# The first attention of a twelve-block network: which operand is stationary in the product with the values

## The chip, the cores and the metric

The kernel runs on one core of a Trainium2 chip. The metric is the time of one execution on the device in microseconds (us), lower is better. The core has a matrix engine (TensorE, in profiles PE, with its weight loads shown apart as PEld), three engines for element-wise work (VectorE or DVE, ScalarE or ACT, GpSimd or POOL), and a queue for transfers (SyncE or SP). A matrix multiplication has a stationary operand, which is loaded into the array as weights, and a moving one, which is streamed through it; the result goes to PSUM.

## The reference

A stream `x` of 4 batches, 128 tokens and 128 features passes twelve residual blocks. The change is in the first, which attends from the tokens to 4 x 2048 context rows. Cut to what matters here (`bitnet_linear` multiplies quantized activations by ternary weights):

```python
vis = bitnet_linear(dinov2_features, W_d2v, b_d2v)             # the context, (4, 2048, 96)
image_embeds = bitnet_linear(vis, W_img, b_img)                # (4, 2048, 128)
fused = bitnet_linear(text_embeddings, W_txt, b_txt)           # the normalized stream, (4, 128, 128)
for Wa, ba in ((W_att0, b_att0), (W_att1, b_att1)):
    kv = bitnet_linear(image_embeds, Wa, ba)                   # 64 features
    k = jnp.concatenate([kv, kv], axis=-1)
    scores = jnp.einsum('bse,bpe->bsp', fused, k) * inv_sqrt_e
    attn = jax.nn.softmax(scores, axis=-1)
    fused = fused + 0.1 * jnp.einsum('bsp,bpe->bse', attn, k)
avg_img = jnp.mean(image_embeds, axis=1, keepdims=True)
concatenated = jnp.concatenate([fused, jnp.broadcast_to(avg_img, (b, s, e))], axis=-1)
h = jax.nn.relu(bitnet_linear(concatenated, W_f1, b_f1))
return bitnet_linear(h, W_f2, b_f2)
```

Keys and values are the same 64 features, used twice side by side to make 128.

## The kernel before, in words

The program is written with a tile framework: each block is a Python method, each engine has an instruction queue that is worked in order, and buffers come from pools that reuse a tag's buffers in turn. A reader of a buffer therefore holds up whoever is given that buffer next. A scheduler settles the order of the instructions of one engine from the order of the code.

`bit_attention` (L771) is the first block. L819 to L897 quantize and project the context. For each round r they leave in one large tile `kv` the keys `kT` (64 features of even and odd chunks of 128 keys on the two halves of the partitions, L886 to L890) and the values `v`: per chunk of 128 keys 64 columns and a 65th column of ones, which L875 sets on GpSimd (once per round) and which L896 leaves alone when it copies the 64 columns out of PSUM.

The attention then runs over eight units (`Unit`, L899), two rounds times four batches. A unit has these steps:

- `queries` (L909): L911 folds the two halves of `fused` on TensorE, L913 scales the result to `fq` on VectorE, L914 adds a bias to `fused`.
- `scores(g)` (L918), for the two halves g = 0, 1 of the keys: 8 products of keys and queries (L924), two at a time on the two halves of the array's rows, into a PSUM tile `st` of 128 keys x (8 chunks x 128 queries); L926 takes the maximum over the chunks on VectorE.
- `top` (L928) and `spread` (L935): L929, L931 and L933 take the maximum over all keys and partitions, by way of a transpose on TensorE; L936 is the second transpose, which spreads it; ScalarE copies the result to `mb` (L938).
- `weights(g)` (L940): VectorE subtracts the maximum out of PSUM (L942), ScalarE takes the exponential in place (L944). The probabilities `p`, with keys on partitions, come from a pool of three buffers.
- `values` (L947): 16 products (L953), one a chunk of keys. The probabilities of a chunk, 128 keys x 128 queries, are the stationary operand and the chunk's 65 columns of values and ones move through. The result `av` has queries on partitions, and its 65th column holds the sum of the weights. L957 takes the reciprocal of that column (128x1), L959 multiplies and doubles the columns, L961 transposes on TensorE and L962 adds to `fused`.

L969 to L995 set the order: in step i the code takes the maximum of unit i, the first half of the scores of unit i+1, the exponentials of unit i, the products with the values of unit i-1, the second half of the scores of unit i+1, and the queries of unit i+2. In step 2 the ternary weights of the later layers are made (`ternary`, L790, whose temporaries L804 have the tag `qtmp` in a pool of two buffers). In steps 3 and 4 one half of a mask each is read by a transfer (L989, into a tile of the same tag `qtmp`) and converted on GpSimd (L992, 3 partitions of 4096 columns). The small PSUM tiles of all these steps (`fq_ps`, `m_tr`, `av`, `o_tr`) share one tag `mm` with two buffers; the score tiles have three.

After the last unit, L1002 takes the largest magnitude of `fused`; its last step is a reduction over the partitions on GpSimd (L749, `am_f_g`)[...]. The program changes the library[...] (in the trace, a pair of MODIFY_POOL_CONFIG records at L341, L749 and L992).

Of the kernel before, what the change touches and what calls it, by code (L numbers as in the profile page):

```python
# [9 lines left out]
F32 = mybir.dt.float32  # L10
# [4 lines left out]
ALU = mybir.AluOpType  # L15
# [3 lines left out]
P = 128  # L19
B = 4  # L20
T = 128
# [3 lines left out]
NS = B * S  # L25
DC = 96
NCH = S // P
# [233 lines left out]
def bc_mid(ap, n):  # L261

    return ap.unsqueeze(1).to_broadcast([ap.shape[0], n, ap.shape[1]])
# [7 lines left out]
class Net:  # L271
# [499 lines left out]
    def bit_attention(self, nxt):  # L771


        nc, tc = self.nc, self.tc
        w = self.load("l0x")
        with ExitStack() as es:
            one = es.enter_context(tc.tile_pool(name="bit1", bufs=1))
            wk = es.enter_context(tc.tile_pool(name="bit2", bufs=2))
            big = es.enter_context(tc.tile_pool(name="bit_big", bufs=2))
            BIG = NS // 2 + B * NCH * 65  # L780
            qp = es.enter_context(tc.tile_pool(name="bit_q", bufs=1))
            tp = es.enter_context(tc.tile_pool(name="bit_t", bufs=3))

# [30 lines left out]
            ps = es.enter_context(tc.tile_pool(name="bit_ps", bufs=2, space=PSUM))  # L814
# [29 lines left out]
            total = one.tile([P, NS // W], F32, name="total")  # L844
# [24 lines left out]
            HC = NCH // 2  # L869
            rounds = []  # L870
            for r, n in enumerate(("att0", "att1")):
                kv = big.tile([P, BIG], F32, tag="big", name="kv")
                kT = kv[:, 0 : NS // 2]
                v = kv[:, NS // 2 :].rearrange("p (c w) -> p c w", w=65)
                nc.gpsimd.memset(v[:, :, 64:65], 1.0)  # L875
                osc = out_scale(n, s_img)
                osc10 = self.small(1, "osc10" + n)
                nc.vector.tensor_scalar_mul(osc10, osc, 0.1)
                rounds.append((n, kT, v, osc10))
                pairs = qimg.rearrange("p (c h k) -> p c h k", h=2, k=P)  # L880
                for j in range(B):
                    mm = stp.tile([P, W], F32, tag="st", name="k_ps")
                    for lo in range(0, W, 512):
                        at = (j * W + lo) // P
                        for h in range(2):
                            nc.tensor.matmul(  # L886
                                mm[h * 64 : h * 64 + 64, lo : lo + 512], qw[:, L0X[n]], pairs[:, at : at + 4, h],
                                start=True, stop=True)
                    nc.scalar.activation(
                        kT[:, j * W : j * W + W], mm, AF.Identity, bias=self.col("b_" + n), scale=osc)  # L890
                    mm = stp.tile([P, W], F32, tag="st", name="v_ps")
                    for i in range(NCH):
                        at = (j * NCH + i) * P
                        nc.tensor.matmul(
                            mm[:, i * 64 : i * 64 + 64], qimg[:, at : at + P], qw[:, L0X[n]], start=True, stop=True)
                    nc.vector.tensor_copy(  # L896
                        v[:, j * NCH : j * NCH + NCH, 0:64], mm.rearrange("p (c w) -> p c w", w=64))  # L897

            class Unit:  # L899

# [8 lines left out]
                def queries(u):  # L909
                    mm = ps.tile([P, 512], F32, tag="mm", name="fq_ps")  # L910
                    nc.tensor.matmul(mm[:, 0:T], self.flat(fold), u.fb, start=True, stop=True)  # L911
                    u.q = wk.tile([P, T], F32, tag="fq", name="fq")
                    nc.vector.tensor_scalar_mul(u.q, mm[:, 0:T], 1.0 / math.sqrt(C))  # L913
                    nc.vector.scalar_tensor_tensor(  # L914
                        u.fb, self.col("b_" + u.n).to_broadcast([P, T]), 0.1, u.fb, ALU.mult, ALU.add)
                    u.mh = wk.tile([P, 2, P], F32, tag="mh", name="mh")

                def scores(u, g):  # L918
                    u.st[g] = stp.tile([P, 2, HC // 2, P], F32, tag="st", name="st")
# [20 lines left out]
                def weights(u, g):  # L940
# [3 lines left out]
                    nc.scalar.activation(p, p, AF.Exp)  # L944
                    u.ts.append(p)

                def values(u):  # L947
                    av = ps.tile([P, 512], F32, tag="mm", name="av")
                    for g in range(2):
                        for h in range(2):  # L950
                            for c in range(HC // 2):
                                ch = u.b * NCH + 2 * (g * (HC // 2) + c) + h
                                nc.tensor.matmul(  # L953
                                    av[:, 0:65], u.ts[g][:, h * (HC // 2) + c], u.v[:, ch],
                                    start=g + h + c == 0, stop=g + h == 2 and c == HC // 2 - 1)
                    r = self.small(1, "rsum")
                    nc.vector.reciprocal(r, av[:, 64:65])  # L957
                    o = wk.tile([P, 2, 64], F32, tag="o", name="o")
                    nc.vector.tensor_scalar(o, bc_mid(av[:, 0:64], 2), r, u.osc10, ALU.mult, ALU.mult)  # L959
                    mm = ps.tile([P, 512], F32, tag="mm", name="o_tr")  # L960
                    nc.tensor.transpose(mm[:, 0:P], self.flat(o), self.ident)  # L961
                    nc.vector.tensor_add(u.fb, u.fb, mm[:, 0:P])  # L962

            units = [Unit(r, b) for r in range(2) for b in range(B)]
            units[0].queries()
# [969 lines left out]
```

## Time and profile before

| What | Value |
|---|---|
| median of 3 runs | 1716.02 us (1714.92 to 1716.68) |
| the profiled execution | 1714.14 us, of which the span 1712.3 us |
| TensorE busy | 1267.0 us, 74% of the span |
| VectorE, ScalarE, GpSimd busy | 1004.9, 624.2 and 140.3 us |
| L953, products with the values | 256 records, 52.9 us busy |
| L924, scores | 256 records, first at 82.4 us, last at 170.4 us |
| GpSimd between 93.2 and 181 us | two instructions, 7.5 us (L992) |

The profile is of one execution. Its page gives the busy time of each engine in forty equal slices; the chain of waits follows back from the last instruction what each one waited for; the timeline gives instructions in order of time, with how many of a kind follow one another; and a row of a group has a line of the code, the engine, the operation, what is written and read, the shape, the count, the busy time and the mean duration in ns. For a matmul, "128*64 128x512" means 128 rows and 64 columns of the array in use, and 512 columns streamed on 128 partitions. The windows view has for each stretch its length, then busy time and number of instructions for PE, PEld, DVE, ACT and POOL, then the clock that TensorE was granted (1.00 is full), the share of the transfer engines and GB/s.

The stage of the change in that view:

| Stretch, us | PE busy | DVE busy | granted clock |
|---|---|---|---|
| 93.2 to 97.5 | 4.30 | 1.57 | 0.87 |
| 104.5 to 111.7 | 7.20 | 3.58 | 0.50 |
| 134.5 to 141.5 | 7.00 | 3.52 | 0.50 |
| 155 to 162 | 6.11 | 3.15 | 0.50 |
| 181 to 188 | 6.91 | 0.34 | 0.50 |

### The profile page before, as it was taken

To read this page: it belongs to the slowest core of one execution; us is meant where nothing else is said; L and a number is where in the kernel's file an instruction comes from. 1 tells how busy PE (TensorE), PEld (TensorE's weight loads), DVE (VectorE), ACT (ScalarE), POOL (GpSimd) and SP (SyncE) were. 2 spreads that over 40 slices of the span, in tenths; PEclk is the share of its full clock that TensorE was granted. 3 is DMA by queue.
4 is the path that set the end of the run, shared out by engine and by line. 5 is a ranking of instruction groups with operands and counts; after the bars stand their busy time and mean duration, and the time that the engine had idled before them with its cause. 6 is when DMAs were issued, how large, how long until landed. Compare 5 with 4: busy or idle time off the path is not lost.

```text
span 1712.3 us, 15537 instructions
## 1 busy us (share of the span) xinstructions
PE 1267.0 (74%) x6142; PEld 675.3 (39%) x6142; DVE 1004.9 (59%) x1568; ACT 624.2 (36%) x796; POOL 140.3 (8%) x108
## 2 busy tenths in 40 slices
PE   2689547676999999999547155989658328899867
PEld 0378412224434444444213033744225214554544
DVE  8964468993256767676567843124448565444335
ACT  3722255552155656465333012315214202343332
POOL 0010014561000000000001000000012010000000
PEclk9965558798589999999759567959779558898878
DMA  5000000005000000000010004010000000000010
GB/s 153 1 1 1 0 0 5 21 1 155 1 24 1 0 1 1 0 1 1 0 49 1 0 0 123 5 36 0 0 2 1 9 0 1 1 2 2 6 47 7
DMA packets 9372, 28.19 MB, mean 16 GB/s; under 512 B 1176, under 2 KB 7105, under 8 KB 8143
## 3 DMA queue, kind: packets, MB, share of 16 engines
q1 hardware_dynamic: 8174, 24.88, 5.0%
q10 hardware_dynamic: 1120, 2.27, 0.4%
q8 instruction: 50, 0.82, 0.2%
q14 instruction: 28, 0.22, 0.0%
HBM read 26.88 MB, written 0.26 MB: 16 GB/s over the span
## 4 chain that ended last, share of the span: by engine, by line
PE 63%; DVE 24%; ACT 5%; issue 3%; POOL 3%; DMA 1%; POOLq 0%; ACTq 0%; DVEq 0%
PE av L518 12%; PE sc L492 12%; PE s_ps L638 3%; DVE na_m L643 3%; PE mm L1282 3%; PE av L953 3%; PE t_ps L662 3%; PE q_ps L438 2%; DVE h L1199 2%; PE h_ps L1631 2%; PE av L675 2%; PE y_ps L1638 2%; PE y_ps L1204 2%; PE st L924 2%; POOL hc L1202 1%
## 5 line engine op out<-in xcount | busy, mean ns | idle before, releaser
L518 PE MATMUL av<-s,ctx 128*97 128x512 f32 x448 | 211.1, 629 | 19.4 <-ACT s L516 19.3
L492 PE MATMUL sc<-q_aug,ctxT 99*128 99x512 f32 x448 | 207.5, 607 | 1.8 <-DVE q_aug L439 1.8
L494 ACT COPY s<-sc 128x1024 f32<-128x1024 f32 x112 | 113.0, 1010 | 95.2 <-PE sc L492 95.2
L518 PEld LDWEIGHTS av<-s,ctx 128*97 128x97 f32 x448 | 76.6, 174 | 146.9 <-issue 109.0
L515 DVE TENSOR_TENSOR s<-s,mbs 128x1024 f32<-128x1024 f32 x112 | 128.9, 1220 | 4.8 <-ACT mbs L512 4.8
L643 DVE TENSOR_REDUCE na_m<-s_ps 128x2 f32<-128x1024 f32 x64 | 75.7, 1220 | 89.2 <-PE s_ps L638 89.1
L492 PEld LDWEIGHTS sc<-q_aug,ctxT 99*128 99x128 f32 x448 | 83.8, 195 | 96.3 <-issue 79.2
L516 ACT ACTIVATE s<-s 128x1024 f32<-128x1024 f32 x112 | 113.5, 1053 | 10.8 <-DVE s L515 8.2
L498 DVE TENSOR_TENSOR m<-m,s 128x1024 f32<-128x1024 f32 x72 | 88.1, 1223 | 21.9 <-ACT s L494 20.7
L1204 PE MATMUL y_ps<-hc,consts 128*128 128x512 f32 x128 | 75.3, 723 | 33.6 <-POOL hc L1202 30.7
L668 ACT ACTIVATE p<-t_ps 128x1024 f32<-128x1024 f32 x64 | 62.1, 1021 | 91.3 <-PE t_ps L662 91.2
L529 DVE RECIPROCAL rsum<-y 128x2 f32<-128x2 f32 x40 | 6.6, 166 | 133.5 <-PE y L526 133.5
L1202 POOL TENSOR_TENSOR hc<-h,cs 128x1024 f32<-128x1024 f32 x32 | 77.5, 2431 | 86.3 <-DVE h L1199 86.0
L1199 DVE TENSOR_TENSOR_SCAN h<-dA,dbu 128x512 f32<-128x512 f32 x64 | 74.4, 1204 | 3.6 <-ACT dA L1196 3.4
L638 PE MATMUL s_ps<-kT,q 32*128 32x512 f32 x256 | 66.7, 734 | 1.9 <-ACT p L668 1.0
L341 POOL TENSOR_TENSOR ln_sq<-ln_xc 128x512 f32<-128x512 f32 (+1 forms) x19 | 23.3, 1225 | 537.9 <-DVE ln_xc L339 537.9
L662 PE MATMUL t_ps<-q,kT 32*128 32x128 f32 x1024 | 54.5, 319 | 8.8 <-DVE na_m L643 5.8
L1204 PEld LDWEIGHTS y_ps<-hc,consts 128*128 128x128 f32 x128 | 26.0, 222 | 83.2 <-POOL hc L1202 57.0
L662 PEld LDWEIGHTS t_ps<-q,kT 32*128 32x128 f32 x1024 | 45.0, 215 | 26.4 <-DVE na_m L643 14.7
L1196 ACT ACTIVATE dA<-delta,A 128x508 f32<-128x508 f32 x64 | 42.7, 688 | 33.1 <-DVE h L1199 32.2
L953 PEld LDWEIGHTS av<-kv,p 128*128 128x128 f32 x256 | 53.2, 319 | 0.2 <-issue 0.2
L953 PE MATMUL av<-kv,p 128*128 128x65 f32 x256 | 52.9, 399 | 0.0
(574 smaller groups left out, 2084.4 us busy)
## 6 DMA issues: line engine op xcount, KB each, us to landing
w_moe<-in_moe SPq DMA_DIRECT2D x2, 2048.0 KB, 8.0
ctxT<-in_ctxT SPq DMA_DIRECT2D x4, 768.0 KB, 14.7
rows<-in_rows ACTq DMA_DIRECT2D x1, 2048.0 KB, 11.8
w_l3f<-in_l3f SPq DMA_DIRECT2D x1, 1920.0 KB, 7.9
w_l0f<-in_l0f SPq DMA_DIRECT2D x1, 1024.0 KB, 4.8
w_mamba<-in_mamba SPq DMA_DIRECT2D x1, 976.0 KB, 20.5
w_r<-in_r SPq DMA_DIRECT2D x1, 960.0 KB
consts<-in_consts SPq DMA_DIRECT2D x1, 832.0 KB, 18.6
```

The costliest lines, as they stand in the source:

```text
L492: nc.tensor.matmul(sc[:, i], self.ctxT[:, at : at + P], qg, start=True, stop=True)
L494: nc.scalar.copy(s, sc)
L515: nc.vector.tensor_sub(p, p, bc_mid(mbs, 2))
L516: nc.scalar.activation(p, p, AF.Exp)
L518: nc.tensor.matmul(av[: DC + 1], self.ctx[:, b * NCH + chunks[j + i]], p[:, i], start=j + i == 0, stop=j + i == n - 1)
L638: nc.tensor.matmul(ts[g // 2][:, g % 2], qs[lo : lo + 32], kT[lo : lo + 32, s, j * 512 : j * 512 + 512], start=True, stop=True)
L643: nc.vector.tensor_reduce(part[:, at : at + 2], t, axis=AX, op=ALU.max, negate=True)
L662: nc.tensor.matmul(ts[g // 2][:, g % 2, j], kT[g * 32 : g * 32 + 32, s, at : at + P], qs[g * 32 : g * 32 + 32], start=True, stop=True)
L953: nc.tensor.matmul(av[:, 0:65], u.ts[g][:, h * (HC // 2) + c], u.v[:, ch], start=g + h + c == 0, stop=g + h == 2 and c == HC // 2 - 1)
L1199: nc.vector.tensor_tensor_scan(h[:, half], self.flat(dA), dbu[:, half], 0.0, ALU.mult, ALU.add)
L1202: nc.gpsimd.tensor_mul(hc, h, bc_mid(cs, 2))
L1204: nc.tensor.matmul(y[:, half], self.ident, hc[:, half], start=n == 0, stop=n == 15)
```

## The change

In `values` the operands swap places. A chunk's 64 columns of values become the stationary operand, and the probabilities move, 128 columns at a time. The product has features on partitions and queries along the free axis; chunks of h = 0 are summed on the lower 64 columns of the array, those of h = 1 on the upper 64, and the two alternate. The ones column and the two memsets that set it are gone, and with them 65 becomes 64 in the layout of `v`.

The sums of the weights are now made in two steps. In `weights`, three additions on GpSimd for each half g reduce the eight chunks of `p` to one 128x128 tile `total` (512, 256 and 128 columns; the intermediate has the tag `qtmp`). In `values`, two products with a matrix of ones sum `total` over the keys; every partition then holds the sums of all queries. The reciprocal is taken of this 128x128 tile, multiplied by `av`, and a product with `fold` adds the two halves of the columns and repeats the result on both halves of the partitions, so that no transpose is needed. The last instruction scales and adds to `fused`. In the scheduled order of TensorE, the transpose of the maxima (L931) now stands ahead of the first half of the next scores, where before two of those eight products stood ahead of it.

```diff
-            BIG = NS // 2 + B * NCH * 65
+            BIG = NS
...
-                v = kv[:, NS // 2 :].rearrange("p (c w) -> p c w", w=65)
-                nc.gpsimd.memset(v[:, :, 64:65], 1.0)
+                v = kv[:, NS // 2 :].rearrange("p (c w) -> p c w", w=64)
...
+                u.total = wk.tile([P, 2, P], F32, tag="total", name="total")
...
                     nc.scalar.activation(p, p, AF.Exp)
                     u.ts.append(p)
+                    half = p[:, 0 : HC // 2]
+                    a = wk.tile([P, HC // 2, P], F32, tag="qtmp", name="psum")
+                    nc.gpsimd.tensor_add(a, half, p[:, HC // 2 :])
+                    nc.gpsimd.tensor_add(a[:, 0:2], a[:, 0:2], a[:, 2:4])
+                    nc.gpsimd.tensor_add(u.total[:, g], a[:, 0], a[:, 1])
...
                 def values(u):
                     av = ps.tile([P, 512], F32, tag="mm", name="av")
                     for g in range(2):
-                        for h in range(2):
-                            for c in range(HC // 2):
+                        for c in range(HC // 2):
+                            for h in range(2):
                                 ch = u.b * NCH + 2 * (g * (HC // 2) + c) + h
                                 nc.tensor.matmul(
-                                    av[:, 0:65], u.ts[g][:, h * (HC // 2) + c], u.v[:, ch],
-                                    start=g + h + c == 0, stop=g + h == 2 and c == HC // 2 - 1)
-                    r = self.small(1, "rsum")
-                    nc.vector.reciprocal(r, av[:, 64:65])
-                    o = wk.tile([P, 2, 64], F32, tag="o", name="o")
-                    nc.vector.tensor_scalar(o, bc_mid(av[:, 0:64], 2), r, u.osc10, ALU.mult, ALU.mult)
-                    mm = ps.tile([P, 512], F32, tag="mm", name="o_tr")
-                    nc.tensor.transpose(mm[:, 0:P], self.flat(o), self.ident)
-                    nc.vector.tensor_add(u.fb, u.fb, mm[:, 0:P])
+                                    av[h * 64 : h * 64 + 64, 0:T], u.v[:, ch], u.ts[g][:, h * (HC // 2) + c],
+                                    start=g + c == 0, stop=g == 1 and c == HC // 2 - 1)
+                    mm = ps.tile([P, 512], F32, tag="mm", name="rsum")
+                    for g in range(2):
+                        nc.tensor.matmul(mm[:, 0:T], self.ones, u.total[:, g], start=g == 0, stop=g == 1)
+                    o = wk.tile([P, T], F32, tag="o", name="o")
+                    nc.vector.reciprocal(o, mm[:, 0:T])
+                    nc.vector.tensor_mul(o, o, av[:, 0:T])
+                    nc.tensor.matmul(mm[:, T : 2 * T], self.flat(fold), o, start=True, stop=True)
+                    nc.vector.scalar_tensor_tensor(u.fb, mm[:, T : 2 * T], u.osc10, u.fb, ALU.mult, ALU.add)
```

In the changed kernel the lines of this part are: the additions L949 to L951, the products with the values L960, the products with ones L965, the reciprocal L967, the multiplication L968, the fold L969 and the last addition L970. The lines ahead of them that the text names (L910 to L944) move by at most one, the mask conversion is L1000.

More of the change, by code (lines that the diff above doesn't have):

```diff
@@ L896, in bit_attention @@
                     nc.vector.tensor_copy(
-                        v[:, j * NCH : j * NCH + NCH, 0:64], mm.rearrange("p (c w) -> p c w", w=64))
+                        v[:, j * NCH : j * NCH + NCH], mm.rearrange("p (c w) -> p c w", w=64))
             class Unit:
```

## The prediction

> **What bounds the kernel now.** I read the page's slices first, then the chain of waits of the stretch that the change touches, then its timeline and the clock in windows. The change touches only the first attention, from 88 to 190 us of a span of 1712.3 us. In the page's slices (42.8 us each) that is the third to the fifth:
>
> ```profile
> PE   2689547676999999999547155989658328899867
> DVE  8964468993256767676567843124448565444335
> POOL 0010014561000000000001000000012010000000
> PEclk9965558798589999999759567959779558898878
> ```
>
> There TensorE is busy 80 to 90%, VectorE about half, GpSimd idle, and the granted clock is 0.5. The chain of waits over one unit (one of eight: two rounds by four batches):
>
> ```profile
> 134.40 0.40 PE m_tr L936
> 134.80 6.73 PE av L953 x32
> 141.53 2.03 PE st L924 x16
> 143.59 1.23 DVE mh L926
> 144.81 0.19 DVE fused L962
> 145.00 0.21 DVE fq L913
> ...
> 145.26 0.80 PE st L924 x4
> 146.06 0.40 PE m_tr L931
> 146.46 1.58 PE st L924 x12
> 148.04 0.40 PE m_tr L936
> ```
>
> A unit lasts 13.64 us (134.40 to 148.04) and 12 us of it are TensorE at half clock; half the unit is the product with the values, L953. Its timeline row, one window of the clock inside it, and the rows of another attention that already works the way the change does:
>
> ```profile
> 148.24 6.93 PE L953 MATMUL av<-kv,p 128*128 128x65 f32 x32
> ```
> ```profile
> 148.91:152.32 3.41, 3.41 (x18) 3.41 (x18) 2.06 (x3) 1.06 (x1) 0.00 (x0) 0.50 0.03 5
> 1505.17:1508.58 3.41, 3.29 (x72) 2.32 (x70) 1.36 (x2) 1.85 (x2) 0.00 (x0) 1.00 0.00 0
> ```
> ```profile
> 1506.56 1.07 PE L675 MATMUL av<-p,v 128*17 128x128 f32 x32
> ```
>
> An f32 matmul of the program is two records (passes). A full-array pass of 512 columns takes 0.43 us at full clock (L610, four in 1.98 us less the 0.27 us that the last needs to drain), so 128 columns take 0.107, or 0.213 at half clock. L953 streams 65 columns and still takes 6.93/32 = 0.217 us: it is paced by loading 128 columns of probabilities as weights, and streams half of the time. L675 streams 128 columns against 17 value columns on four column strips: (1.07 - 0.27)/32 = 0.025 us a pass, a quarter of 0.107, so the strips run together.
>
> [...] every stretch of one clock is a multiple of 3.41 us, but for the last, which the end cuts. [...] L341's library is called at 201.10 and its first multiply starts at 207.89, 6.79 later, 0.89 us after its input is ready instead of the usual 0.08 to 0.15.
>
> What counts as activity I worked out of the records: for each window, the sum of passes x streaming time at full clock x the shares of rows and columns they use, over 3.41 us. After 77 us, of 282 windows at full clock, 34 of the 36 with 0.385 or less were followed by half clock, and none of the 246 above; of 194 at half clock, none of the 145 below 0.375 was followed by full, and 31 of the 35 at 0.40 or more were. So about 0.39 decides, both ways. L953 at half clock gives 0.25: it can't leave half clock. A unit holds 32 x 0.054 (L953) + 32 x 0.107/2 (L924, half the rows) + 0.21 (L911) + 0.32 (three transposes) = 3.98 us, and 3.98/13.64 = 0.29.
>
> **The change part by part.**
> - Products (L960): 32 passes of 128 columns, two at once: 32 x 0.107/2 = 1.71 us at full clock, 3.41 at half, against 3.5 and 6.93. At half clock it keeps the array full (0.5 in a window), over the threshold.
> - Row sums (L965): 4 passes, +0.43 or 0.85 us on TensorE. The fold L969 (0.21 or 0.43) replaces the transpose L961 (0.47 with its drain): nothing. One more change of tile shape, about 0.2 us (the gaps put down to issue).
> - VectorE: the reciprocal goes from 128x1 to 128x128. Its rows bound it:
>
> ```profile
> L1379 DVE RECIPROCAL Di<-dec 128x512 f32<-128x512 f32 x1 | 3.4, 3353 | 0.0
> L1708 DVE RECIPROCAL rs<-sums 128x64 f32<-128x64 f32 x1 | 0.6, 554 | 0.0
> ```
>
>   Between them 128x128 is 0.55 + 64 x 6.25 ns = 0.95 us, +0.79. Multiply and fused add (0.28 each) replace L959 and L962 (0.41 and 0.28).
> - GpSimd: three adds per half unit. From L1626 (128x512, 1.26 us) and the rows of L341 (1.03 at 512, 3.60 at 2048): 1.26 + 0.72 + 0.44 and 0.1 between them, 2.65 us; L1389's rows for these sizes (1.6, 0.84, 0.72) give 3.4 as the upper end. Two of them finish about 9.0 us after L936 (10.5 at the upper end); L965 wants them 1.9 us into the next unit, at 10.3. L965 stands in TensorE's queue before the scores, so lateness stops everything; cover is 1.3 us, and -0.2 at the upper end. The two mask conversions (L1000, 3.76 us each) now stand among the adds and use up that cover around units 3 to 5: up to 0.5 us, inside the range.
> - Shared buffers: masks and ternary temporaries share the tag with the adds. L805 now waits for unit 2's adds, which end (9.0) about when it is reached (8.9); the mask DMAs wait for adds too and leave after w_dtp on SP instead of before it, all wanted much later. The two memsets (0.21 and 1.09 us) lay beside work: nothing.
> - Order: L931 now stands before the next scores instead of among them, and waits for L970, which frees its PSUM buffer: in the sum below.
>
> One unit at full clock, from L936: maximum of the scores 1.22 (to 1.34), two subtractions (to 3.77), with products, row sums and scores under them (scores to 3.7); reciprocal to 4.72; maximum to 5.94; multiply 6.2; fold, fq and fused add to 7.0; fq copy 7.25; scores to 8.35: **8.4 us**. VectorE is the bound. At half clock: products and sums to 4.6, scores to 6.8, maximum to 8.07, then the same steps with 2.1 us of scores: **12.1 us**; there the reciprocal is hidden.
>
> The stage at full clock. L936 of unit 0 to unit 1: 26 passes of the product lie in it, -1.2. From there to L936 of unit 7 (96.63 to 174.28, 77.65 us): 7.7 (its first maximum is done ahead of L936) + 8.4 + (8.4 + 3.7 for L798 to L806, which hold up unit 3 on VectorE) + 8.4 + 8.4 + 8.0 (no more queries) = 53.0, so -24.65. Tail: before, am_f_g starts 16.2 us after the last exponentials' L936. After, the second exponential ends at 4.4, the adds at 8.45, then GpSimd changes its library (L749), at least 6.0: am_f_g at 14.6 to 15.3. The PE and VectorE path alone would need 13. So the tail gains only 1.2. In all -27.
>
> Does the clock stay full? A unit now holds 1.71 + 1.71 + 0.43 + 0.21 + 0.21 + 0.21 = 4.48 us, 0.53 of 8.4. But TensorE idles from 3.7 to 6.3, and a window that begins 2.2 to 4.7 us into a unit holds under 0.385: 30% of windows, 2.46 windows a unit, 0.73 drops a unit. Products, sums and scores (6.4 us in one piece at half clock) always bring it back. A drop costs 1.4 half windows and about 1.5 us; over six units -1.1 each is taken off: 27 - 6.5 = 20.5. So 1714.14 - 20.5 = 1693.6 us for the profiled execution (span 1712.3 and 1.84 around it); the median of the runs is 1.9 above it: **1695.5**.
>
> **Rivals.**
> 1. Full clock throughout: -27, 1689. For: mean activity 0.53. Against: the idle 2.6 us.
> 2. Half clock throughout: units of 12.1 (0.37 on average), 70.2 instead of 77.65, 0.5 at the start, 1 in the tail: -9, 1707. For: before, the clock fell at 101 us. Against: the 6.4 us dense piece.
> 3. Slower: the two column halves run one after the other. Place L960; price 3.4 us a unit at half clock, which then persists (0.25 of a window): 15.5 us a unit, +10, and +4 in the tail: 1730. It decides once a pass costs more than 0.156 us at half clock (0.107 if they overlap, 0.213 if not). For: nothing in the trace has two f32 strips of 64. Against: L675 with four, and L886's bf16 halves (four passes of 512 columns in 0.62 us, where 0.85 would be serial).
> 4. GpSimd's adds late by contention as in L1202's worst (3.25 against 2.35 us): 3.7 us each, 0.8 a unit, 5 us: 1700, within the range.
>
> **How the numbers follow.** Forecast, with 4 in it, 61%; rival 1 12%; rival 2 15%; rival 3, or another loss of the kind, 12%. Range 1686 (full clock, 28 to 29 gained, quickest adds) to 1709 (half clock with the adds late). 0.2% is 3.4 us, about what a measurement here tells from nothing. Faster 0.86, same 0.02, slower 0.12.
>
> **What would show it.** L960: 32 passes in about 1.9 us at full clock, 3.6 at half. Clock of the stage mostly 1.0. L967 near 0.95 us. L949 to L951 together 2.4 to 3.1. L936 to L936 8.4 to 10 us. am_f_g at least 6 us after the last L951. It is wrong if L960 takes over 0.15 us a pass, if the clock stays 0.5, or if L965 waits for GpSimd in most units.

## The result, and the profile after

The changed kernel takes 1691.22 us (median of 4 runs, 1689.8 to 1696.29), against 1715.47 for the kernel before on the same chip: ratio 0.987, 95% interval 0.9841 to 0.9899. Predicted were 1695.5. The profiled execution took 1691.67 us, its span 1689.4, which is 22.9 less than before.

The slices of the page (42.2 us each) that answer to those of before; the third and fourth are the stage:

```profile
PE   2666556768999999998465336899658238889867
DVE  8877588972276676766568743225448565454335
POOL 0046033650000000000001000000011100000000
PEclk9978568897599999999768667959769558898768
```

There TensorE is now in its sixties of per cent and VectorE in its seventies, GpSimd is in its forties and then its sixties, and the clock has gone from 0.6 and 0.5 to 0.7 and 0.8. The time between the first L936 and `am_f_g` (L749) can be split at the starts of L936:

| Stretch | before, us | after, us | difference | predicted difference |
|---|---|---|---|---|
| L936 of unit 0 to unit 1 | 8.7 | 8.6 | 0.0 | -1.2 |
| unit 1 to unit 7 | 77.7 | 56.5 | -21.2 | -18.2 |
| unit 7 to `am_f_g` | 16.2 | 14.2 | -2.0 | -1.2 |
| sum | 102.6 | 79.3 | -23.3 | -20.6 |
| of it at half clock | 93.0 | 27.3 | | |

Outside of it nothing of note happened: the first L936 starts 0.5 us earlier, and what follows `am_f_g` is 0.8 longer. So the whole gain is in the stage, nearly all in the eight units. The windows view, cut where the clock changes, shows how (columns: stretch and length, then busy time and count of PE, PEld, DVE, ACT and POOL, clock, transfers):

```profile
95.30:102.12 6.82, 4.33 (x47) 3.36 (x43) 4.83 (x7) 2.38 (x3) 3.21 (x6) 1.00 0.01 2
102.12:108.95 6.83, 6.61 (x52) 5.57 (x51) 4.95 (x7) 1.72 (x3) 2.71 (x4) 0.50 0.00 0
108.95:122.60 13.65, 8.03 (x96) 6.61 (x96) 12.40 (x21) 3.04 (x4) 5.89 (x8) 1.00 0.01 2
122.60:129.43 6.83, 6.35 (x44) 5.39 (x46) 4.36 (x10) 0.41 (x2) 6.49 (x6) 0.50 0.01 2
129.43:143.08 13.65, 9.45 (x113) 7.65 (x109) 12.25 (x19) 4.35 (x5) 11.93 (x12) 1.00 0.01 3
143.08:146.50 3.42, 3.42 (x28) 2.94 (x29) 2.54 (x4) 0.27 (x1) 2.12 (x3) 0.50 0.00 0
```

Where the old form fell to half clock and stayed there, the new one falls three times between unit 1 and unit 7 (96.2 to 152.8 us) and comes back after one or two windows. Look at PE: in the half-clock rows it is 93 to 100% busy, in the full-clock rows 59 to 69%. By the prediction's measure (full-clock work as a share of a 3.41 us window) the windows ahead of a return held 0.42 to 0.48, those ahead of the three falls about 0.25: the clock comes back where TensorE is dense at half clock, and falls where it is not dense at full. The products, from the timeline, at half and at full clock:

```profile
105.20 3.68 PE L960 MATMUL av<-p,kv 128*64 128x128 f32 x32
136.39 1.97 PE L960 MATMUL av<-p,kv 128*64 128x128 f32 x32
```

and the chain of waits over the first 6.6 us of a unit of 9.0, at full clock; the old unit was 12 us of TensorE out of 13.6:

```profile
136.25 0.57 DVE mh L926
136.82 0.57 issue
137.40 0.16 DVE p L942
137.56 0.97 issue
138.53 1.22 DVE p L942
139.74 0.86 DVE o L967
140.61 1.08 DVE mh L926
141.68 0.20 DVE o L968
141.88 0.04 issue
141.92 0.50 PE rsum L969 x2
...
142.45 0.36 DVE fused L970
```

At full clock the chain runs through VectorE. In the two longer stretches put down to "issue", VectorE was at work as well: by the timeline its instructions L926, L942, L967, L926 and L968 follow one another without a gap from 136.25 to 141.87.

What a total tells of one part is limited here. Executions of the same kernel differ by some us (1689.8 to 1696.29 for the changed one), and so does what follows the stage (1519.9 to 1530.5 us in the profiles below, for the same instructions). That the same work falls differently into the windows of the clock is the likely cause; no run shows it alone. Where parts are compared, the text therefore uses the profiled stage, "first L936 to `am_f_g`", beside the median.

### The profile page after: what moved, and what is told of

It reads as the page before. It is cut to its first block, busy times and chain, and to the rows that moved or that the text cites. A ratio compares the mean times of both kernels' runs of the same rounds, so it can differ in the third digit from the quotient of the medians.

```text
span 1689.4 us, 15676 instructions
## 1 busy us (share of the span) xinstructions
PE 1235.2 (73%) x6182; PEld 642.0 (38%) x6182; DVE 1012.7 (60%) x1568; ACT 624.3 (37%) x796; POOL 178.1 (11%) x154
## 4 chain that ended last, share of the span: by engine, by line
PE 61%; DVE 25%; ACT 5%; issue 4%; POOL 3%; DMA 1%; POOLq 0%; ACTq 0%; DVEq 0%
PE av L518 12%; PE sc L492 12%; PE s_ps L638 4%; DVE na_m L643 3%; PE mm L1290 3%; PE t_ps L662 3%; PE q_ps L438 2%; DVE h L1207 2%; PE h_ps L1639 2%; PE av L675 2%; PE y_ps L1646 2%; PE y_ps L1212 2%; POOL hc L1210 1%; PE o_ps L1711 1%; POOL ln_sq L341 1%
## 5 line engine op out<-in xcount | busy, mean ns | idle before, releaser
L341 POOL TENSOR_TENSOR ln_sq<-ln_xc 128x512 f32<-128x512 f32 (+1 forms) x19 | 23.3, 1227 | 537.6 <-DVE ln_xc L339 537.6
L358 PE MATMUL tr_xnT<-consts,xn 128*128 128x128 f32 x32 | 8.7, 428 | 60.0 <-DVE xn L348 41.2
L522 ACT COPY oT<-av 97x512 f32<-97x512 f32 x20 | 11.7, 586 | 109.1 <-PE av L518 109.1
## 6 DMA issues: line engine op xcount, KB each, us to landing
ctxT<-in_ctxT SPq DMA_DIRECT2D x4, 768.0 KB, 13.5
```

## The experiments

In edited kernels the lines move by some; the text gives the numbers that the lines have in the kernel before (L953, products) and in the changed one (L913, L929, L949 to L970), and says so where a fence shows others.

### Is it the clock? The kernel before, with wider streaming

The first test leaves the change out altogether. It takes the kernel before and lets L953 stream 128 columns instead of 65: work whose result nobody reads, in time that the pass takes anyway (at half clock the 32 passes of a unit took 6.93 us with 65 columns, and 6.97 with the 88 of a later test).

```diff
-                                    av[:, 0:65], u.ts[g][:, h * (HC // 2) + c], u.v[:, ch],
+                                    av[:, 0:128], u.ts[g][:, h * (HC // 2) + c], u.v[:, ch * 65 : ch * 65 + 128],
```

> The kernel before, with 128 columns moving in L953 instead of 65 (the 63 more are the next chunks' values; their results are not read). Nothing else is changed: the order, the number of passes and the weight loads stay. Theory A (the clock is decided by the share of the array in use per window, and the old form was caught at half clock by streaming only 65 of the 128 columns' time that a pass lasts): a pass still takes 0.217 us at half clock, but a window of L953 now holds 0.5 of full-clock work instead of 0.25, so the clock comes back to full. Unit 1 to unit 7 (L936 to L936) falls from 77.65 us to between 58 and 68, and the time from 1715 to between 1697 and 1707 us. Theory B (the gain of the change is the fewer TensorE cycles of the swapped product and nothing about the clock): nothing gets shorter: clock 0.5, 77 to 79 us, 1714 to 1718 us.

Measured: 1688.13 us, ratio 0.9868 (0.9815 to 0.9921), as much as the change brought, and 9 us below theory A's range. First L936 to `am_f_g` is 78.6 us (before 102.6, after 79.3), unit 1 to unit 7 is 60.0, and 23.9 us of the stage are at half clock instead of 93.0. Added work on the busiest engine took 24 us off. Theory B falls: the swap's fewer TensorE cycles are not needed for a gain of this size, since the old product with a fuller array has it too.

If a threshold per window decides, a little more streaming should do nothing for a clock that has fallen, and a little more than that everything. Two widths stand on the two sides of 0.39:

> The kernel before, with 88 columns moving in L953 instead of 65 (23 more columns of the next chunk's values; their results are not read). Passes, loads and order stay. A window that lies in L953 at half clock holds 0.25 of full-clock work at 65 columns, so 0.25 x 88/65 = 0.339 here. Theory A (a threshold of about 0.39 per 3.41 us window decides): too little, the clock does not come back once it has fallen: over 80 us at half clock between the first L936 and am_f_g, this stretch at 95 to 103 us (before 102.6), time 1708 to 1718 us. Theory B (any more streaming helps by degrees): a third of the way to the 78.6 us of 128 columns, 93 to 96 us.

> As the run with 88 columns, with 108: 0.25 x 108/65 = 0.415 in a window that lies in L953 at half clock. Theory A (threshold of about 0.39): enough, every half-clock window inside L953 is followed by full clock: 20 to 40 us at half clock in the stage, first L936 to am_f_g 78 to 84 us (78.6 with 128 columns, 102.6 before), time 1686 to 1698 us. Theory B (by degrees): two thirds of the way, 86 to 88 us, 1697 to 1701.

The edit is that of the first test with 88 and 108 in place of 128. The windows view of a window that lies within the products (here L955) and of the one after it, first with 88 columns:

```profile
126.13:129.54 3.41, 3.41 (x18) 3.41 (x17) 2.02 (x3) 1.06 (x1) 0.00 (x0) 0.50 0.00 0
129.54:132.95 3.41, 3.41 (x18) 3.25 (x19) 1.19 (x3) 1.06 (x1) 0.00 (x0) 0.50 0.00 0
```

then with 108:

```profile
117.19:120.60 3.41, 3.41 (x18) 3.41 (x18) 0.75 (x1) 0.00 (x0) 2.71 (x1) 0.50 0.04 8
120.60:124.01 3.41, 2.26 (x26) 1.89 (x24) 2.82 (x5) 1.73 (x3) 3.41 (x2) 1.00 0.00 0
```

The first window of each is 100% busy with the same 18 passes at half clock. After the one of 88 columns the clock stays 0.50; after the one of 108 it rises. "Busy" does not decide, then: the share of the array's work does (0.34 and 0.43 by the records). With 88 columns the clock fell at 119.3 us and no window lifted it for the rest of the stage, 69.3 us at half clock, and a unit took 13.69 us, where before it took 13.65. With 108 every half-clock window inside the products was followed by full clock, 20.5 us were at half clock, and the stage took 75.0 us, less than the 78 to 84 of theory A; the time was 1686.14 us, ratio 0.9823 (0.9802 to 0.9845), where it had 1686 to 1698.

With 88 columns theory A missed its numbers: 69.3 us at half clock (over 80 expected), a stage of 94.2 us (95 to 103), and 1698.6 us (1708 to 1718). The stage happens to lie where theory B put it, but the mechanism is not B's: the stage is not evenly a third better. The clock held from 95.4 to 119.3 us, and then the kernel was as slow as before. The four runs are two near 1706, one of them the profiled one, and two at 1685.9 and 1691.7. What theory A had left out is that streaming more also fills the windows at full clock: those from 95.4 us on held 0.41 to 0.65, until one of 0.34 was followed by half clock. The kernel before has such runs as well: of its 33 runs beside these experiments three took 1694.7 to 1695.4 us, the others 1706.7 to 1721.5. They have no profile; that the clock held in this stage in those three is likely, and not shown.

### Do the two column halves run together?

The order of the loops was changed so that the 16 passes of one half of the columns don't alternate with the other's; here eight passes of the lower 64 columns are followed by eight of the upper.

```diff
-                        for c in range(HC // 2):
-                            for h in range(2):
+                        for h in range(2):
+                            for c in range(HC // 2):
```

> The changed kernel, but the 16 products with the values of a half unit go first all to the lower 64 columns of the array and then all to the upper 64, so neighbours in TensorE's queue do not use different columns. Theory A (neighbours on different columns stream together, and half of L960's speed is this): a pass goes from 0.053 to 0.107 us at full clock, L960 from 1.97 to about 3.7 us; its windows hold only 0.25 to 0.27 of full-clock work, so the stage falls back to half clock for most of its time, with L960 at 6.9 us; unit 1 to unit 7 is 75 to 95 us against 56.5, and the time 1710 to 1730 us. Theory B (a pass of 64 columns is short for another reason, as a cheaper weight load): no change, L960 under 2.2 us at full clock, 1689 to 1694 us.

Measured, from the timeline:

```profile
134.32 2.57 PE L960 MATMUL av<-p,kv 128*64 128x128 f32 x32
```

2.57 us lies between the two theories (under 2.2 and about 3.7). In the single records passes start 0.109 us apart at first; 6 ns after the fifth another one starts, and from there two rows of passes run side by side, each at its 0.109. The records don't name the column half, but two on the same half can't be 6 ns apart when such passes take 0.109. In the changed kernel two passes start 7 ns apart, and pairs every 0.109 us. So the halves do run together, and, if the spacing is read rightly, TensorE starts passes of the next half while three of the earlier one still wait; the order cost 0.6 us and not the 1.7 of theory A. The stage took 77.7 us (79.3 in the changed kernel), the time 1694.85 (1689.33 to 1702.21): a product 0.6 us longer per unit left no mark there. This profile had 17.0 us at half clock instead of 27.3, so what the order costs at the same clock stays open.

### What GpSimd's additions cost

Without them:

```diff
-                    nc.gpsimd.tensor_add(a, half, p[:, HC // 2 :])
-                    nc.gpsimd.tensor_add(a[:, 0:2], a[:, 0:2], a[:, 2:4])
-                    nc.gpsimd.tensor_add(u.total[:, g], a[:, 0], a[:, 1])
...
-                        nc.tensor.matmul(mm[:, 0:T], self.ones, u.total[:, g], start=g == 0, stop=g == 1)
+                        nc.tensor.matmul(mm[:, 0:T], self.ones, u.ts[g][:, 0], start=g == 0, stop=g == 1)
```

> The changed kernel without the additions L949 to L951: L965 takes the first chunk of each half instead of the sum of the eight, so the row sums leave out the other seven chunks. Theory A (GpSimd costs two things: about 2 us in the tail, where its library change after the last addition is not covered, and 0.3 to 1 us a unit where VectorE's small operations with two SBUF inputs, L913 and L929, stand still while an addition runs): the tail from the last L936 to am_f_g falls from 14.2 to 12 to 13 us, L929 and L913 never exceed 0.35 us, unit 1 to unit 7 falls from 56.5 to 52 to 55 us, and the time by 3 to 6 us to 1685 to 1688. Theory B (GpSimd is covered everywhere but in the tail): unit 1 to unit 7 stays within 0.7 us of 56.5, and the time falls by 1 to 2.5 us.

The row sums leave out seven chunks of eight here. It was not faster: 1699.38 us (1693.8 to 1701.03), ratio 0.991 (0.9877 to 0.9943) beside 0.987 for the changed kernel, intervals that overlap. The stage was 83.5 us, unit 1 to 7 62.2, with 35.5 us at half clock. Only the tail was as expected (13.0). Both theories missed what its timeline shows:

```profile
118.19 7.51 POOL L994 TENSOR_SCALAR ctxT<-mask,consts 3x4096 f32<-3x4096 uint8 x2 [56.47 <-DMA mask<-in_mask]
122.28 3.56 DVE L928 TENSOR_TENSOR mh<-mh 128x128 f32<-128x128 f32 x1
```

L928 (the L929 of the changed kernel) takes 3.56 us instead of 0.28: with no additions in front of them, the two mask conversions on GpSimd stand back to back until 125.70, and the small maximum ends 0.14 us after. How much of the longer stage is this and how much the clock, the run does not separate. In the changed kernel the same happens with the additions:

```profile
133.05 1.27 POOL L949 TENSOR_TENSOR psum<-p 128x512 f32<-128x512 f32 x1
133.31 1.16 DVE L929 TENSOR_TENSOR mh<-mh 128x128 f32<-128x128 f32 x1
```

L949 ends at 134.32, L929 at 134.47. L913 and L929 have both operands in SBUF. In every case in the traces in which one of them took over 0.5 us (31) it ends 0.14 or 0.15 us after a GpSimd instruction; L926 and L942, which read PSUM, keep their 1.22 us while GpSimd runs. So VectorE stood still in L913 and L929 until the running GpSimd instruction had ended; why, no trace shows. The groups of the changed kernel in the stage add it up; 8 and 6 times 0.28 would be 2.2 and 1.7 us:

```profile
L929 DVE TENSOR_TENSOR mh<-mh 128x128 f32<-128x128 f32 x8 | 3.9, 487 | 0.1
L913 DVE SCALAR_TENSOR_TENSOR fused<-cols,fused 128x128 f32<-128x128 f32 x6 | 3.8, 631 | 0.0
```

The test of that: keep the additions and take these two operations away from VectorE.

```diff
-                    nc.vector.scalar_tensor_tensor(
-                        u.fb, self.col("b_" + u.n).to_broadcast([P, T]), 0.1, u.fb, ALU.mult, ALU.add)
+                    nc.scalar.activation(u.fb, u.fb, AF.Identity, bias=u.b10)
...
-                    nc.vector.tensor_max(u.mh[:, 0], u.mh[:, 0], u.mh[:, 1])
...
-                    nc.tensor.transpose(u.mm[:, 0:P], u.mh[:, 0], self.ident)
+                    for g in range(2):
+                        nc.tensor.transpose(u.mm[:, g * P : g * P + P], u.mh[:, g], self.ident)
                     u.mq = self.small(1, "mq")
-                    nc.vector.reduce_max(u.mq, u.mm[:, 0:P], axis=AX)
+                    nc.vector.reduce_max(u.mq, u.mm[:, 0 : 2 * P], axis=AX)
```

> The changed kernel without the two small VectorE operations of a unit that read two operands in SBUF: L913 (bias) goes to ScalarE, and L929 (maximum of the two halves) is replaced by a second transpose ahead of the maximum over 256 columns. Theory A (VectorE stands still in L913 and L929 until the running GpSimd operation ends; 0.84, 0.57, 1.16, 0.62 and 1.25 us instead of 0.28 in the changed kernel): nothing of VectorE's small operations exceeds 0.45 us in the stage, whatever GpSimd runs; VectorE loses 0.56 us a unit less 0.15 for the wider maximum, and 3 us of standing still; first L936 to am_f_g falls from 79.3 to 72 to 77 us, the time by 2 to 6 us, to 1685 to 1689. Theory B (the standing still is hidden behind TensorE, or the clock decides alone): 78 to 81 us, no change of time.

Measured: the stage 75.5 us, inside the 72 to 77 of theory A, and 1689.73 us (1686.56 to 1693.74), 0.7 above its range; the total alone does not tell it from the changed kernel (ratio 0.9849, 0.9827 to 0.987). None of the operations that each unit repeats is stretched any more; two of the small ones:

```profile
L934 DVE TENSOR_REDUCE mq<-m_tr 128x1 f32<-128x256 f32 x8 | 3.4, 422 | 2.4 <-PE m_tr L932 2.4
...
L969 DVE TENSOR_TENSOR o<-o,av 128x128 f32<-128x128 f32 x8 | 2.2, 277 | 0.0
```

L969 (L968 of the changed kernel), with one operand in SBUF and one in PSUM, has its 0.28 in all runs. Two operands in SBUF are not the whole of it, though: L801 of the ternary weights, 128x2 from SBUF to SBUF with one tile read, took 0.70 us here instead of 0.16 and ended 0.03 us after an addition, which theory A (nothing over 0.45 us) had excluded. It or its like, L799, was held so in five of the runs with additions; why, the traces do not say. The stage gained 3.8 us by the edit. Of that, 2.7 lie between units 0 and 1, where this profile is at full clock and that of the changed kernel at half; units 1 to 7 gained 1.1. That L913 and L929 stand still until a GpSimd instruction ends (the 31 cases over 0.5 us, up to 3.56 instead of 0.28) is plain in the traces; what it costs alone stays open between 1 and 4 us.

### The drops of the clock, and the reciprocal

Two steps of the prediction said what a unit at full clock costs: VectorE bounds it, and each drop of the clock adds to it. Fillers were to keep the clock up:

```diff
+                    for k in range(4):
+                        nc.tensor.matmul(u.rs[:, 2 * T : 4 * T], self.ones, u.ts[1][:, 0:2], start=True, stop=True)
```

> The changed kernel with four more matmuls of 256 columns a unit on the full array, whose results are not read, put where TensorE waits for VectorE (one lands ahead of the last score products, three between them and the fold). Theory A (the windows at half clock in units 2 to 5 cost what full clock would have saved, and they come from TensorE's idle time there): a unit holds 4.48 + 1.7 = 6.2 us of full-clock work in 8.4 us, no window falls below 0.39 between 97 and 150 us, the clock there is 1.00, unit 1 to unit 7 falls from 56.5 to about 53 to 54.5 us, and the time by 2 to 4 us. Theory B (VectorE bounds these units at either clock): the clock rises but unit 1 to unit 7 stays at 56 to 57 us, or grows by the fillers in the way of the scores, 0.43 us each.

The clock did rise (22.7 us at half instead of 27.3, none from 92.7 to 120.0), but the stage took 84.1 us and the time was 1699.47. From 94.3 to 112.4 us all was at full clock, and the units took 8.34 and 9.76 us there, only 0.2 and 0.1 less than the 8.55 and 9.9 of the changed kernel with two half-clock windows among them. That speaks for theory B, though the fillers' own time is in it. In the worst unit, 13.2 us, the standing still took its part again: a mask conversion met L913, which took 2.68 us.

```profile
133.42 3.76 POOL L1012 TENSOR_SCALAR ctxT<-mask,consts 3x4096 f32<-3x4096 uint8 x1
134.64 2.68 DVE L913 SCALAR_TENSOR_TENSOR fused<-cols,fused 128x128 f32<-128x128 f32 x1
```

So the run does not give a price for a drop alone. The reciprocal of 128x128 was replaced by one of 128x1 and a transpose that spreads it:

```diff
-                        nc.tensor.matmul(mm[:, 0:T], self.ones, u.total[:, g], start=g == 0, stop=g == 1)
+                        nc.tensor.matmul(mm[:, 0:1], u.total[:, g], self.ones[:, 0:1], start=g == 0, stop=g == 1)
...
-                    nc.vector.reciprocal(o, mm[:, 0:T])
+                    nc.vector.reciprocal(r, mm[:, 0:1])
+                    nc.tensor.transpose(mm[:, 2 * T : 3 * T], r.to_broadcast([P, P]), self.ident)
+                    nc.scalar.copy(o, mm[:, 2 * T : 3 * T])
```

> The changed kernel with the row sums taken per query: L965 with the totals stationary and one column of ones moving, a reciprocal of 128x1 (0.17 us instead of 0.95), a transpose of it spread over 128 columns, a copy on ScalarE, then the multiplication as before. Theory A (at full clock VectorE bounds a unit, and the 0.79 us of the wider reciprocal are on its path): 0.5 to 0.8 us a unit, 4 to 6 us from first L936 to am_f_g (79.3 to 73 to 76), and 3 to 6 us of the time. Theory B (the reciprocal lies in a wait for the scores or in half-clock time): within 1.5 us of 79.3, no change of time; the transpose and the copy in the tail cost about 0.7 us.

81.0 us and 1696.59 us (1694.7 to 1701.58), beside 1694.1 for the changed kernel measured with it: no gain, theory B. Its chain shows a reason: the transpose (here L968) now stands ahead of the last scores on TensorE, so the maximum with which VectorE goes on waits for both.

```profile
109.35 0.87 PE st L924 x12
110.22 0.25 PE rsum L968
110.47 0.45 PE st L924 x4
110.92 0.02 issue
110.94 1.23 DVE mh L926
```

The 0.78 us saved on VectorE became a wait for TensorE. The clock had a share too: 33.2 us of this stage were at half clock, against 27.3 and 27.4 in the two profiles of the changed kernel. The prediction's "VectorE is the bound" holds for the order of the changed kernel, and not with 0.8 us to spare.

### The tail

The prediction had GpSimd's change of library as the end of the tail. The changed kernel's timeline:

```profile
160.63 0.45 POOL L951 TENSOR_TENSOR total<-psum 128x128 f32<-128x128 f32 x1
164.75 0.15 DVE L746 TENSOR_REDUCE am_f_m<-am_f_m 128x1 f32<-128x2 f32 x1
166.95 0.38 POOL L749 PARTITION_ALL_REDUCE am_f_g<-am_f_m  x1 [5.87 <-issue]
```

L749 starts 5.87 us after the last addition, and 2.05 us after its input is there. What the prediction calls the change of library shows here as two MODIFY_POOL_CONFIG records of L749, the second at 161.3, 5.6 us ahead of it. With the last unit's additions on VectorE:

```diff
+                    e = nc.vector if u is units[-1] else nc.gpsimd
-                    nc.gpsimd.tensor_add(a, half, p[:, HC // 2 :])
+                    e.tensor_add(a, half, p[:, HC // 2 :])
```

(and likewise for the other two)

> The changed kernel with the last unit's additions L949 to L951 on VectorE; the other seven units' stay on GpSimd. Theory A (GpSimd's library change after the last addition is what am_f_g waits for at the end): the change of library moves to before the end and is covered; am_f_g starts within 0.3 us of its input L746, and 11.5 to 13 us after the last L936 instead of 14.2; the rest of the stage is as in the changed kernel; time 1 to 3 us less. Theory B (VectorE's additions, about 2 us, stand in its way instead, or the clock is half there): 13.5 to 15 us, no change.

```profile
158.28 0.80 PE L970 MATMUL rsum<-o,fold 128*128 128x128 f32 x2 [2.81 <-DVE o L969]
159.00 3.68 PE L961 MATMUL av<-p,kv 128*64 128x128 f32 x32
162.61 1.22 PE L966 MATMUL rsum<-total,ones 128*128 128x128 f32 x4
163.88 0.96 DVE L968 RECIPROCAL o<-rsum 128x128 f32<-128x128 f32 x1 [4.42 <-PE rsum L966]
```

GpSimd was out of the way (L749 started 0.14 us after its input), and the tail was 15.5 us, longer than 14.2 and beyond even the 13.5 to 15 of theory B; the time, 1693.28 us (1692.03 to 1695.46), was no less. Theory B is right in both of its parts. The additions, 2.7 us of VectorE, stood ahead of the multiplication and fold of the unit before (here L969 and L970), for which TensorE waited 2.81 us with the last products behind it, and those then ran at half clock. With only the second half's additions on VectorE, and L913 and L929 off it:

> The changed kernel with L913 and L929 off VectorE, and of the last unit only the second half's additions on VectorE, so that GpSimd has ended its additions about 4 us earlier and its library change is covered. Theory A (in the run with all of the last unit's additions on VectorE these, 3.1 us, held up the fold of the unit before and with it the buffers of the last products): half of that, 1.4 us, holds it up less: last L936 to am_f_g falls from 14.2 to 12 to 13.7 us, first L936 to am_f_g from 75.5 to 73 to 75.5; time 1684 to 1689 us. Theory B (TensorE at half clock bounds the tail): 14 to 15.5 us, the time as with L913 and L929 alone (1689.7).

Stage 73.0 us, tail 12.4, time 1683.89 us (1679.78 to 1685.5), ratio 0.9813 (0.9791 to 0.9834); as theory A had it, the time just below its 1684. Here the last products ran at full clock, so how much of the 15.5 us was VectorE's queue and how much the half clock is not told apart. L749 still starts 0.7 us after its input there, and 6.15 after the last addition on GpSimd.

### A kernel without the change

If the clock was what the change bought, the kernel before should need no swap, no additions on GpSimd and no wide reciprocal: 108 columns in L953, and L913 (L914 in the kernel before) and L929 off VectorE (the edits shown above).

> The kernel before with two edits alone: 108 columns moving in L953, and the small VectorE operations L913 and L929 taken off VectorE as in the run without them. Nothing of the change is in it. Theory A (the clock is what the change bought, so that a kernel without the change that keeps the clock is at least as fast as the changed one): 1682 to 1688 us, at or below the changed kernel in the same call; first L936 to am_f_g 71 to 76 us (75.0 with 108 columns alone). Theory B (the fewer TensorE cycles of the swapped product matter too): 2 us or more above the changed kernel.

> The changed kernel itself, unchanged, beside these three on the same chip. Both theories: 1689 to 1696 us. If the place of the 3.41 us windows relative to the work is what differs from run to run, the profiled stage has the same 256 products and the same operations, but half-clock windows at other places than in the first profile, and the time from first L936 to am_f_g differs from 79.3 by up to 4 us.

| Kernel, side by side on one chip | median, us | range | first L936 to `am_f_g` | at half clock |
|---|---|---|---|---|
| before | 1714.81 | 1711.65 to 1719.74 | no profile | no profile |
| changed kernel again | 1694.1 | 1688.84 to 1696.99 | 78.8 | 27.4 |
| changed, L913 and L929 off VectorE, tail | 1683.89 | 1679.78 to 1685.5 | 73.0 | 17.1 |
| before with 108 columns, L913 and L929 off VectorE | 1681.56 | 1679.61 to 1686.03 | 67.0 | 3.4 |

The last is faster than the kernel before and the changed one: ratio to before 0.981 (0.979 to 0.9831), and all five of its runs lie below all five of the changed kernel. Theory A had it slower than it is (1682 to 1688 us, a stage of 71 to 76). The totals do not tell it from the third row, since their ranges overlap; only the stages, of one profile each, are 6 us apart. Its windows view has one clock in 52 us:

```profile
88.00:100.00 12.00, 9.43 (x89) 7.79 (x87) 10.53 (x14) 6.73 (x9) 0.00 (x0) 1.00 0.00 1
100.00:110.00 10.00, 8.98 (x91) 7.90 (x92) 8.02 (x17) 2.78 (x4) 0.00 (x0) 1.00 0.00 0
110.00:120.00 10.00, 7.92 (x80) 7.10 (x80) 8.96 (x13) 3.05 (x5) 6.57 (x2) 1.00 0.02 6
120.00:130.00 10.00, 9.20 (x89) 8.25 (x89) 8.10 (x12) 3.26 (x5) 0.95 (x1) 1.00 0.01 2
130.00:140.00 10.00, 9.20 (x92) 7.97 (x90) 7.40 (x12) 4.42 (x6) 0.00 (x0) 1.00 0.00 0
```

TensorE is 79 to 92% busy there and keeps its clock, and the units last 7.6 to 9.1 us. The changed kernel's second profile has, as expected, half-clock windows at other places, and nearly the same sum of them.

## Why the prediction was right

- **The bound and its cure.** Half clock held up by low activity was the step that carried the sum, and the widths 88, 108 and 128 show it: the same passes, the same loads, another clock. The threshold of 0.39 stood between 0.34 and 0.43 as foretold. The swap is one way to fill the windows, and not the only one.
- **Products, sums, reciprocal, additions.** L960 took 1.97 and 3.68 us (1.9 and 3.6 foretold), L967 0.95, the three additions 1.27, 0.73 and 0.46. These sizes were right.
- **Rival 3** (column halves one after the other) is out by the records of pairs. What passes that are wholly serial would have cost, no run shows.
- **Drops of the clock.** Foretold 0.73 a unit, 4.4 over six units, from windows that begin 2.2 to 4.7 us into a unit (every beginning equally likely, an estimate); there were three, from windows that begin 2.5, 4.5 and 3.5 us into theirs. The cause was right, the price is the term that was mis-sized. The prediction took 6.5 us off for them (-24.65 to -18.2 between units 1 and 7); measured is -21.2, so all that was lost there against the full-clock sum is 3.5 us, and this holds the standing still of L913 and L929 too. That a half-clock window costs little where VectorE is the slower engine anyway fits this, and no run shows it alone.
- **A cost left out.** VectorE's waits for GpSimd, 3.8 us of busy time in the stage. Rival 4 looked for contention in the other direction, GpSimd made late; L949 stayed at 1.26 to 1.32 us in the changed kernel. With a price for the drops that was too high and these waits put at nothing, two errors of opposite sign met in one sum: that the units came within 3 us is in part luck.
- **Unit 0 to 1.** Foretold -1.2, measured 0.0: 88.5 to 95.3 us was at half clock, which the sum had at full.
- **The tail.** Foretold 14.6 to 15.3 us, set by a library change of at least 6.0 (an estimate from the 6.79 and 0.89 us of L341); measured 14.2 and 5.87. Right in kind, 0.8 us off. The path over TensorE and VectorE was ready at 12.1 (13 foretold).
- **Together**: 1.2 lost at the start, 3.0 won in the units, 0.8 in the tail make about the 2.7 us by which the stage gained more than foretold. The time was 4.3 us less than the forecast; of the rest, the forecast had put its median 1.9 us above the profiled execution, as it lay before, and this time it lay 0.45 below.
- **What the sum could not see** is that the swap itself was not needed. With L913 and L929 off VectorE its stage took 75.5 us, 19.7 of it at half clock; that of the old product with 108 columns took 67.0, with 3.4 at half clock. In these two profiles the old one keeps the clock better, and its tail, with no additions on GpSimd ahead of L749, is 11.7 us against 14.2. At the very same clock the two were not compared.
- **Slips in its working**, without weight for the sum: in the slices, TensorE is at 50% in the fifth and the clock at 0.6 in the third; rival 3's 3.4 us a unit on top of rival 2's 70.2 us make the six units 13 us longer, not 10; and L953, taken as paced by loading 128 columns, loads 128 rows as well, so it can't tell which of the two sets the load time. L924 tells more: it loads 64 rows of 128 columns, in 0.330 us at half clock, beside 0.333 for L953, so here half the rows took the same time.

## What to carry to other kernels

When a stage sits at half clock with TensorE "busy", compute the work per 3.41 us window (streaming time at full clock, times the used shares of rows and columns) before rewriting anything: if passes are paced by their weight loads, as those of L953 were (0.217 us at half clock for 65 columns), streaming more columns in the same pass may lift the clock; here 18 passes of 108 columns filled a window as 18 of 88 did, and only after those of 108 did the clock rise. Before moving work to an idle GpSimd, list VectorE's operations with two SBUF operands in the same stretch: here two of them, of 0.28 us, took up to 3.56, until a GpSimd instruction had ended. Look in the trace for others, as L801 (0.70 us instead of 0.16); here, reading from PSUM (L934 of the test without L913 and L929, 0.42 us on average) or giving the operation to ScalarE avoided it. In a stage that hovers near the threshold (0.39 here) judge parts by the stage in the trace, since the total of one kernel moved by several us (1688.84 to 1696.99 for the changed one).

## What the runs showed that was not expected

- A window 100% busy in the profile can leave the clock at half: 18 passes of 88 columns did, 18 of 108 did not. What set the two apart is how much of the array's capacity was used, 0.34 and 0.43 of a window.
- An f32 pass on 64 columns alone starts every 0.109 us, and two column halves share that time in part also when they do not alternate in the queue: 32 passes in 1.97 us alternating, 2.57 in groups of eight.
- A 0.28 us operation of VectorE took up to 3.56 us, ending 0.14 us after a 3.76 us GpSimd conversion that writes only 3 partitions: it stood still for the length of an instruction that uses 3 of 128 partitions.
